# Eight layers over 625 nodes in one kernel: waits of the TensorE queue are rearranged, and three rows of the soft mixture go by DMA

## The chip, the cores and the metric

The kernel runs on one core of a Trainium2 chip, as one launch. The time is device time in microseconds (us) from the start to the end of an execution; of several runs the median counts. A core has five engines with an instruction queue each: TensorE (PE, matrix products and transposes), VectorE (DVE), ScalarE (ACT), GpSimd (POOL) and SyncE (SP), which here only issues DMAs. An engine works through its own queue in order and waits on semaphores for the others.

## The reference, cut to what matters

Eight residual layers act on x, 625 nodes by 768 features in float32, over one graph of 5000 drawn edges, their reverses and self-loops. Each layer reads a LayerNorm of x and adds its result to x:

- L0_gnn: graph attention, 12 heads of 64
- L0_ffn: mixture of 8 experts with hidden size 192, each node takes two
- L1_gnn: one graph convolution
- L1_ffn: self-attention with 12 heads and a mixture of 8 experts with biases (top 2)
- L2_gnn: two graph convolutions
- L2_ffn: soft mixture, 4 experts of 1024 slots each
- L3_gnn: two graph attention layers, 4 heads of 512, then one of 768
- L3_ffn: mixture of 8 experts (top 2)

Two pieces are needed below. Graph attention takes, for each target node, the softmax over its edges of a leaky ReLU:

```python
e = jax.nn.leaky_relu(a1[src] + a2[dst], negative_slope=NEG_SLOPE)
m = jax.ops.segment_max(e, dst, num_segments=n)
w = jnp.exp(e - m[dst])
```

The soft mixture takes two softmaxes of the same logits, one over the nodes for each slot (dispatch), one over all slots for each node (combine):

```python
dispatch = jax.nn.softmax(logits, axis=1)
combine = jax.nn.softmax(logits.reshape(B, N, E * S), axis=-1).reshape(B, N, E, S)
slots = jnp.einsum('bnd,bnes->besd', x, dispatch)
```

## The kernel before, in words

The 625 nodes are five tiles of 125 (TILES[t], P = 125, NT = 5); 768 features are six chunks of 128 (KD). x stays in SBUF for the whole kernel. PSUM is one pool of four buffers of two banks each (self.ps()); whoever asks for a fifth waits until the oldest has been read. Weights go through a pool `w` of four buffers; SP loads them in order, each as soon as PE has finished with the buffer. The instructions of each engine are put in order by a scheduler that goes by its own estimates; the order of the calls in the code is its start, and it may move an instruction ahead of others that it doesn't depend on.

**Products.** Nearly every large product is done with seven products of half size in place of eight. `half_products` and `half_nodes`, `right_sums` and `left_sums` make the sums that go in; L401 and L385 (in `half_mm` and `half_rest`) and the `add` of `tile_pair` and `down` take the products out of PSUM, on DVE, with one copy U on ACT (L384, L1178) at the start. So after PE's first product, the next ones need a PSUM buffer that DVE or ACT has read.

**Entering a layer.** `final(t)` adds a bias where there is one and normalises tile t: `ln_tile` takes bn_stats on DVE (L167), bn_aggr (L170), a square root on ACT (L171), a reciprocal (L172), a scale (L174, L180), all into xn. `turned` then transposes xn on PE (L187), and `turn_tile` copies it to xT (L191, or with a scale and a shift per feature L194, six copies on ACT). `late` and `turn_due` hold a tile's transposes back until a later point.

**L0_gnn.** The edge counts are in AT (625 x 625). `log_counts` takes their logarithm, `mask_tile` transposes a tile of AT (five transposes, L531), and ACT makes a mask mb (L534) and the degree (L535) from it. A loop over i (12 heads and 4 more) then runs five steps on different heads: `gat_largest(i)` spreads a row of a1 over all partitions (`spread`: five transposes of a broadcast column, L132), takes on DVE the largest a1 among each target's neighbours (L560, five times) into gat_m, and makes of it on POOL the largest logit gat_u (L565 to L569); `gat_exp(i - 2)` spreads gat_u, subtracts it on DVE (L582) and exponentiates on ACT (L584); `back(i - 4)` and `gather(i - 3)` are PE's products (L118, copied by ACT at L826) and their way out; `score(i)` makes the scores of a head on ACT (L547) and POOL (L551). A small copy on ACT (L813) makes head i's scores wait for gat_m of head i - 1; after the loop L906 makes the copy of the identity wait for the last gat_u.

**The mixtures.** `experts` runs up the hidden chunks c = 0, 2, ... 10 (hg), takes the gates from the router's logits, writes them as 8 rows to DRAM (gD, L1072) and reads each back spread over 128 partitions (L1031, L1034), and multiplies them in (L1041). `gate_parts` (L958 to L965) splits the gates into three bfloat16 parts for the expert biases, only in L1_ffn. `down` multiplies by the second weights: tile 0 alone, then the pairs t = 1 and t = 3 with seven products each, in the order 1, 6, 7, 4, 2, 5, 3. Where another layer follows, `final(0)` stands behind product 6 of t = 1. `beside` runs small steps beside a mixture (in L0_ffn and L1_ffn the attention vectors of L3_gnn: a load av_w on SP and two dot products on DVE, L1354 and L1355): one per c in the loop upwards and seven behind the products of t = 1.

**L2_ffn.** A loop over i (16 pairs of 128 slots; e = i // 4 - 1 is the expert before, q = i % 4) makes the logits of a pair (`front`, seven products, L347), their largest per slot, the exponentials (L1722, on ACT), turns these (L1735) and multiplies (`hidden`). When an expert's four pairs are there, `largest(e)` transposes the running maximum M and reduces it to rm (125 nodes on partitions by 5 tiles by 4 experts, L1765). In the next step, between the products of `front`, `spread(e)` makes a row of it on 128 partitions (five transposes L132, a copy on ACT L1770), `weights(e, q)` subtracts that row from a pair on DVE (L1774) and exponentiates it on ACT, four times, and `combine(e)` multiplies the result by hE (the products of hE and lt, L125).

**L3_gnn.** `narrow` (L268 to L277) makes the attention ends of all heads: products with a narrow matrix, a copy on ACT (L273), five transposes (L276), a reduction on DVE. `project(h)` makes a head's features with `tile_pair`, which takes `between`, a function that runs between its products 1, 2 and 6, 7. `right_sums` here is POOL's for heads 2 and 3.

## Time and profile before

| | us |
|---|---|
| median of 3 runs (lowest to highest) | 1891.52 (1891.14 to 1892.33) |
| the profiled execution | 1890.76 |
| its span, from the first instruction to the last | 1889.0 |
| mean granted TensorE clock in it | 0.985 |

Where the layers lie in the span, and how long PE was busy in each (read from the busy times by stretch; the ends are chosen by hand at the first instructions of the next layer):

| stretch | us | PE busy | PE clock |
|---|---|---|---|
| L0_gnn | 0 to 229 | 191.02 | 0.89 |
| L0_ffn | 229 to 380 | 146.12 | 0.99 |
| L1_gnn | 380 to 450 | 70.00 | 1.00 |
| L1_ffn, attention | 450 to 703 | 248.22 | 1.00 |
| L1_ffn, mixture | 703 to 862 | 151.56 | 1.00 |
| L2_gnn | 862 to 1040 | 178.00 | 1.00 |
| L2_ffn | 1040 to 1400 | 356.47 | 1.00 |
| L3_gnn | 1400 to 1700 | 296.96 | 1.00 |
| L3_ffn | 1700 to 1889 | 183.47 | 1.00 |

How to read the profile lines: a line of the timeline or of a group names the engine, the line of the kernel, the operation, the tile written and the tiles read, the shape and the count. Behind it stands in brackets how long the engine had been idle, and which instruction released it. The list of waits sums the idle time by the pair of waiting line and releaser. "SPq" is SyncE's queue, where a DMA is issued. Matmul ends are modelled, so PE's busy time includes some pipelining. The clock is the share of full TensorE speed that the throttle granted.

### The profile page before, as it was taken

How to read it: one execution, taken by the hardware profiler on the slowest of the kernel's cores; microseconds unless marked ns; L12 is line 12 of the kernel's file. 1: busy time of each engine (PE TensorE's matmuls, PEld its weight loads, DVE VectorE, ACT ScalarE, POOL GpSimd, SP SyncE). 2: the span in 40 equal slices, each digit the busy share in tenths (PEclk: the TensorE clock that was granted, in tenths of full speed). 3: DMA queues.
4: the chain of work that ended last, by engine and by line, in shares of the span. 5: the costliest groups of instructions: out<-in, count | busy, mean ns of one | idle time of the engine just before them, and what ended most of it. 6: DMA issues, size and time to landing. Idle time of an engine off the chain costs nothing.

```text
span 1889.0 us, 21692 instructions
## 1 busy us (share of the span) xinstructions
PE 1821.8 (96%) x8224; PEld 1270.4 (67%) x8224; DVE 1112.4 (59%) x2211; ACT 528.2 (28%) x963; POOL 658.4 (35%) x556
## 2 busy tenths in 40 slices
PE   8969899999999999999999999999999999999998
PEld 7844565555677766655555778878767888556765
DVE  8789856547566765674936464555756555144452
ACT  2479721002254533100110131322314233111200
POOL 0079665234410044743106322231235321401551
PEclk9968999999999999999999999999999999999999
DMA  2040142210200024414420211001011122021321
GB/s 70 22 145 34 40 116 70 78 58 27 92 25 26 1 70 153 127 53 140 138 67 34 76 43 59 26 26 34 6 39 35 40 72 67 1 73 52 94 72 33
DMA packets 69637, 115.03 MB, mean 61 GB/s; under 512 B 8189, under 2 KB 38111, under 8 KB 69534
## 3 DMA queue, kind: packets, MB, share of 16 engines
q1 hardware_dynamic: 69274, 113.57, 18.9%
q8 instruction: 65, 1.06, 0.2%
q14 instruction: 38, 0.31, 0.1%
q10 hardware_dynamic: 260, 0.09, 0.0%
HBM read 111.63 MB, written 2.01 MB: 60 GB/s over the span
## 4 chain that ended last, share of the span: by engine, by line
PE 84%; DVE 8%; ACT 2%; DMA 2%; issue 2%; POOL 1%; SPq 0%; ACTq 0%; DVEq 0%; POOLq 0%
PE ps L125 65%; PE ps L118 4%; PE ps L768 2%; PE ps L1889 2%; PE ps L1518 2%; PE ps L1550 2%; PE ps L1537 1%; PE ps L187 1%; POOL gat_w L551 1%; PE ps L132 1%; DVE gat_w L582 1%; PE ps L1735 1%; DMA x<-in_x 1%; PE ps L706 1%; DVE av_junk L1355 1%
## 5 line engine op out<-in xcount | busy, mean ns | idle before, releaser
L327 POOL TENSOR_TENSOR S<-w 128x384 f32<-128x384 f32 x40 | 41.4, 1040 | 401.9 <-PE ps L125 298.9
L125 PE MATMUL ps<-xT,w 128*128 128x313 f32 x480 | 137.6, 427 | 0.7 <-ACT pr L1526 0.7
L125 PE MATMUL ps<-w,xT 128*125 128x384 f32 (+2 forms) x392 | 125.2, 473 | 0.0
L125 PE MATMUL ps<-T,w 128*128 128x313 f32 x408 | 122.0, 430 | 0.9 <-DVE U L401 0.9
L551 POOL TENSOR_TENSOR gat_w<-gat_w,xT 125x625 f32<-125x625 f32 x60 | 86.2, 1469 | 102.8 <-DVE xT L523 96.5
L125 PEld LDWEIGHTS ps<-xT,w 128*128 128x128 f32 x480 | 89.3, 189 | 33.6 <-ACT pr L1526 0.9
L125 PE MATMUL ps<-T,S 128*128 128x313 f32 x348 | 103.8, 432 | 1.7 <-DVE T L307 1.4
L125 PEld LDWEIGHTS ps<-w,xT 128*125 128x125 f32 x392 | 72.8, 188 | 46.2 <-issue 11.1
L125 PE MATMUL ps<-xT,S 128*128 128x313 f32 x336 | 100.9, 429 | 2.1 <-DVE hg L401 2.1
L125 PE MATMUL ps<-w,S 128*125 128x384 f32 x292 | 99.8, 487 | 2.6 <-DVE x L1170 2.6
L125 PEld LDWEIGHTS ps<-T,w 128*128 128x128 f32 x408 | 75.6, 189 | 32.2 <-issue 1.8
L125 PE MATMUL ps<-w,hg 128*125 128x384 f32 x288 | 96.3, 486 | 0.0
L125 PE MATMUL ps<-hh,gat_w 125*125 125x257 f32 (+1 forms) x400 | 89.8, 379 | 0.0
L125 PE MATMUL ps<-w,x2T 128*125 128x384 f32 (+1 forms) x280 | 84.2, 449 | 0.0
L125 PEld LDWEIGHTS ps<-T,S 128*128 128x128 f32 x348 | 64.0, 189 | 28.7 <-ACT lt L355 4.4
L125 PEld LDWEIGHTS ps<-w,S 128*125 128x125 f32 x292 | 54.5, 188 | 42.4 <-DVE x L1170 3.9
L125 PEld LDWEIGHTS ps<-hh,gat_w 125*125 125x125 f32 x400 | 73.4, 187 | 11.3 <-issue 0.4
L125 PEld LDWEIGHTS ps<-xT,S 128*128 128x128 f32 x336 | 62.1, 189 | 26.6 <-POOL hg L1041 2.5
L118 PE MATMUL ps<-gat_w,ft 125*65 125x500 f32 (+1 forms) x240 | 74.9, 471 | 4.4 <-DVE gat_w L582 3.1
L125 PEld LDWEIGHTS ps<-w,hg 128*125 128x125 f32 x288 | 53.6, 188 | 36.6 <-issue 0.6
L1355 DVE CUSTOM_DVE_ANT_0 av_junk<-av_w,av_a 128x512 f32<-128x512 f32 (+1 forms) x80 | 74.1, 926 | 6.4 <-DMA av_w<-in_L_gnn_W 4.1
L560 DVE CUSTOM_DVE_ANT_0 junk<-ps,mb 125x625 f32<-125x625 f32 x85 | 68.5, 806 | 13.9 <-PE ps L132 9.9
(459 smaller groups left out, 3794.7 us busy)
## 6 DMA issues: line engine op xcount, KB each, us to landing
w<-in_L_ffn_phiT SPq DMA_DIRECT2D x8, 1536.0 KB
w<-in_L_gnn_W SPq DMA_DIRECT2D x8, 1536.0 KB
gate<-gD SPq DMA_DIRECT2D x24, 312.5 KB
w<-in_L_ffn_w SPq DMA_DIRECT2D x6, 1152.0 KB
w<-in_L_gnn_W SPq DMA_DIRECT2D x6, 1152.0 KB
av_w<-in_L_gnn_W SPq DMA_DIRECT2D x24, 256.0 KB
av_w<-in_L_gnn_W SPq DMA_DIRECT2D x16, 384.0 KB
w<-in_L_ffn_w SPq DMA_DIRECT2D x3, 1536.0 KB
```

Source lines behind the costliest of these rows:

```text
L118: self.nc.tensor.matmul(pv[:, s, :], lhs[i], rhs[i][:, s, :], start=i == 0, stop=i == n - 1)
L125: self.nc.tensor.matmul(out, lhs[i], rhs[i], start=i == 0, stop=i == n - 1)
L132: self.nc.tensor.transpose(pv[:, t, :], col(t).to_broadcast([P, rows]), self.ident[:P, :P])
L187: nc.tensor.transpose(pv[:, k, :P], src[:, k * 128 : (k + 1) * 128], self.ident[:P, :P])
L327: nc.gpsimd.tensor_tensor(S1, A21, A22, ALU.add)
L551: nc.gpsimd.tensor_tensor(w[:, s, :], w[:, s, :], lc[:, s, :], ALU.add)
L560: nc.vector.tensor_tensor_reduce(self.n3(junk), row, self.n3(mb[:, t, :]), 1.0, -3e38, ALU.subtract, ALU.max, m[:, t : t + 1],)
L768: nc.tensor.matmul(acc[j // 2][:, j % 2, :], ohs[:, TILES[j]], ohd[:, 0:HN], start=c == cs[0], stop=c == cs[-1],)
L1355: nc.vector.tensor_tensor_reduce(junk, wt, row, 1.0, 0.0, ALU.mult, ALU.add, dst)
L1518: nc.tensor.matmul(sv[r][:, s, :], qk[half[r], 0, TILES[t]], self.n3(qk[half[r], 1, :])[:, s, :], start=True, stop=True,)
L1550: nc.tensor.matmul(ov[half[r]], v[:, s, h * DH : (h + 1) * DH], pT[r][:, s, :], start=s == 0, stop=s == NT - 1,)
L1889: nc.tensor.matmul(pv[:, j, :], zTs[t][:, k, :], w2[k // 3][:, k % 3, js], start=k == 0, stop=False,)
```

## The change

The change has these parts:

- `gat_largest`: the four operations on POOL become two on DVE, and a row that was made before can be handed in. L0_gnn spreads head 0's row between the log counts and the mask tiles.
- `ln_tile` gets `behind`: a one-column copy on ACT ahead of the square root, which has to wait for what it reads. `down` hands in a column that is written after U2 (one more small copy on ACT), for t = 1.
- `down` calls `beside` behind its adds, once each (`dots`), once in t = 1 and four times in t = 3, in place of seven times behind t = 1; the loop upwards calls two steps at c = 4 and c = 8.
- `turn_tile` with a scale (only L1_ffn's norms) gives three of the last tile's six copies to DVE.
- `gate_parts` goes from DVE to POOL.
- `right_sums` gets `last`: in L1_ffn's v, the last of the four sums goes to POOL.
- In L2_ffn, `spread` of experts 0 to 2 writes a column set of rm to DRAM and reads it back as a row on 128 partitions, both issued on SP, directly behind `largest`. Expert 3 keeps the transposes.
- `narrow` returns its second half as a function, which runs further back: in L3_gnn's first layer between products 1, 2 and 6, 7 of the second pair, with two mask tiles behind it, in the second layer behind another product.

The diff, cut to its core:

```diff
-    def ln_tile(self, src, dst, scale=None, st=None, act=False):
+    def ln_tile(self, src, dst, scale=None, st=None, act=False, behind=None):
...
         nc.vector.bn_aggr(mv, st)
+        if behind is not None:
+            nc.scalar.copy(rs, behind)
         nc.scalar.activation(rs, mv[:, 1:2], AF.Sqrt, bias=self.eps[:P])
         nc.vector.reciprocal(rs, rs)
         if scale is not None:
...
             nc.scalar.copy(dst[:, :, TILES[t]], pv[:, :, :P])
             return
         for k in range(KD):
+            if t == NT - 1 and k % 2:
+                nc.vector.tensor_scalar(
+                    dst[:, k, TILES[t]], pv[:, k, :P], scale[:, k : k + 1], bias[:, k : k + 1],
+                    ALU.mult, ALU.add,
+                )
+                continue
...
     def narrow(self, pool, chunks, w, cols, dst):
         nc, n, few = self.nc, len(chunks), w
...
         hT = pool.tile([128, N], F32, tag="narrow", name="narrow", bufs=1)
         nc.scalar.copy(self.n3(hT), pv)
-        pv = self.nv(self.ps(), P, 128)
-        for t in range(NT):
-            nc.tensor.transpose(pv[:, t, :], hT[:, TILES[t]], self.ident)
-        nc.vector.tensor_reduce(
-            dst, pv.rearrange("p t (q e) -> p t e q", q=4)[:, :, 0:cols, :], AX.X, ALU.add
-        )
+        def turned():
+            pv = self.nv(self.ps(), P, 128)
+            for t in range(NT):
+                nc.tensor.transpose(pv[:, t, :], hT[:, TILES[t]], self.ident)
+            nc.vector.tensor_reduce(
+                dst, pv.rearrange("p t (q e) -> p t e q", q=4)[:, :, 0:cols, :], AX.X, ALU.add
+            )
+        return turned
...
-    def right_sums(self, T, q, eng=None):
+    def right_sums(self, T, q, eng=None, last=None):
         eng = eng or self.nc.vector
...
         eng.tensor_tensor(T3, B22, B12, ALU.subtract)
         eng.tensor_tensor(T2, T3, B11, ALU.add)
         eng.tensor_tensor(T4, B21, T2, ALU.subtract)
-        eng.tensor_tensor(T1, B12, B11, ALU.subtract)
+        (last or eng).tensor_tensor(T1, B12, B11, ALU.subtract)
         return B11, B21, B22, T4, T1, T2, T3
...
-    def gat_largest(self, pool, mb, a1, a2):
+    def gat_largest(self, pool, mb, a1, a2, row=None):
         nc = self.nc
-        row = self.spread(lambda t: a1[:, t : t + 1], P)
+        if row is None:
+            row = self.spread(lambda t: a1[:, t : t + 1], P)
         m = self.small.tile([P, NT], F32, tag="gat_m", name="gat_m")
         for t in range(NT):
             junk = pool.tile([P, N], F32, tag="junk", name="junk", bufs=1)
...
                 m[:, t : t + 1],
             )
         u = self.small.tile([P, NT], F32, tag="gat_u", name="gat_u")
-        nc.gpsimd.tensor_tensor(u, m, a2, ALU.add)
-        v = self.small.tile([P, NT], F32, tag="gat_v", name="gat_v")
-        nc.gpsimd.tensor_scalar(v, u, 0.8, 0.0, ALU.mult, ALU.max)
-        nc.gpsimd.tensor_scalar(u, m, 0.2, None, ALU.mult)
-        nc.gpsimd.tensor_tensor(u, u, v, ALU.add)
+        nc.vector.scalar_tensor_tensor(u, a2, 0.8, m, ALU.mult, ALU.add)
+        nc.vector.scalar_tensor_tensor(u, m, 0.2, u, ALU.mult, ALU.max)
         return m, u
...
             tmpp = ctx.enter_context(tc.tile_pool(name="g0tmp", bufs=1))
             for s in range(NT):
                 self.log_counts(lc, s)
+            row = self.spread(lambda t: al[:, t, 0, 0:1], P)
             for t in range(NT):
                 self.mask_tile(mb, t, act=True)
             self.prepare(router="L0_ffn_router")
...
             for i in range(H + 4):
                 if i < H:
-                    ms[i], us[i] = self.gat_largest(tmpp, mb, a1[i], a2[i])
+                    ms[i], us[i] = self.gat_largest(
+                        tmpp, mb, a1[i], a2[i], None if i else row
+                    )
                 if 0 <= i - 2 < H:
                     h = i - 2
                     self.gat_exp(
...
         nc, lg = self.nc, self.lg
         r = self.small.tile([P, NT, NEXP], F32, tag="gr", name="gr", bufs=1)
-        nc.vector.tensor_copy(r[:, 0, 0:1], after)
+        nc.gpsimd.tensor_copy(r[:, 0, 0:1], after)
         parts = gb[:, :, 0, 0 : 3 * NEXP].rearrange("p t (e i) -> p t e i", i=3)
...
         for j in range(1, gb.shape[2]):
-            nc.vector.tensor_copy(gb[:, :, j, 0 : 3 * NEXP], gb[:, :, 0, 0 : 3 * NEXP])
+            nc.gpsimd.tensor_copy(gb[:, :, j, 0 : 3 * NEXP], gb[:, :, 0, 0 : 3 * NEXP])
...
                 )):
                     gate(o)
                 if beside and c < NF:
-                    beside(1, hg[:P, c + 1, 0:1])
+                    beside(2 if c in (4, 8) else 1, hg[:P, c + 1, 0:1])
             up_pool.close()
             with tc.tile_pool(name="moedown", bufs=1) as dp:
                 self.down(dp, a[w2], hg, gT3, (b2p, b2n) if b2 else None, after, beside)
...
             x11, x12, x21, x22 = (
                 x[:, o, j * HD : (j + 1) * HD] for o in (t, t + 1) for j in range(2)
             )
+            def dots(n, after):
+                if beside and n in ((5,) if t == 1 else (1, 2, 3, 4)):
+                    beside(1, after[:, 0:1])
             U = pool.tile([P, 2, HD], F32, tag="U", name="U")
             U2, U3 = U[:, 0], U[:, 1]
             prod(1, a1)
             nc.scalar.copy(U2, a1)
+            if after and t == 1:
+                nc.scalar.copy(U3[:, 0:1], U2[:, 0:1])
             add(x11, U2)
+            dots(1, x11)
             prod(6, a2)
             add(U2, U2, a2)
+            dots(2, U2)
             if after and t == 1:
-                self.final(0)
+                self.final(0, behind=U3[:, 0:1])
             prod(7, b1)
             add(U3, U2, b1)
             add(x12, U2)
+            dots(3, x12)
             prod(4, b2, (t + 1, bl))
             if t == 1:
                 sums(3)
...
             if not after:
                 store(t, 0)
             add(x22, U3)
+            dots(4, x22)
             prod(5, a2, (t + 1, br))
             add(x22, a2)
             if not after:
                 store(t + 1, 1)
             add(x12, a2)
+            dots(5, x12)
             prod(3, b1, (t, br), (t + 1, bn))
             add(x12, b1)
...
                 continue
             for o in (t, t + 1):
                 self.final(o, hold=True)
-            if beside and t == 1:
-                beside(7, U3[:, 0:1])
...
                     [wv[j][:, k, :] for k in range(KD)],
                 )
             nc.vector.tensor_tensor(halves(v[:, 0, :]), pv, halves(vb), ALU.add)
-            rights = self.right_sums(vp, columns(wv))
+            rights = self.right_sums(vp, columns(wv), last=nc.gpsimd)
             lefts = {1: self.left_sums(vp, yT, 1, inplace=False)}
...
                     nc.vector.tensor_reduce(rm[:, :, e], tv, AX.X, ALU.max)
                 def spread(e):
-                    bv = self.spread(lambda t: rm[:, t, e : e + 1], 128)
                     rows[e] = mp.tile([128, N], F32, tag="mrow", name="mrow")
-                    nc.scalar.copy(self.n3(rows[e]), bv)
+                    if e == E:
+                        bv = self.spread(lambda t: rm[:, t, e : e + 1], 128)
+                        nc.scalar.copy(self.n3(rows[e]), bv)
+                        return
+                    r = rD[e : e + 1, :]
+                    nc.sync.dma_start(r.rearrange("o (t p) -> p (o t)", p=P), rm[:, :, e])
+                    nc.sync.dma_start(rows[e], r.to_broadcast([128, N]))
+                E = NE - 1
+                dram = c1.enter_context(
+                    tc.tile_pool(name="f2d", bufs=1, space=bass.MemoryType.DRAM)
+                )
+                rD = dram.tile([E, N], F32, name="rD")
                 def weights(e, q):
                     pr = pairs[4 * e + q]
...
                     )
-                E = NE - 1
...
                     o = 2 * i - 2
                     c = [[], [], []]
                     if e >= 0 and q == 1:
-                        c[0] += [(spread, e), (weights, e, 0), (weights, e, 1)]
+                        c[0] += [(weights, e, 0), (weights, e, 1)]
                         c[1] += [(weights, e, 2)]
                         c[2] += [(weights, e, 3)]
                     if 0 < i < LAST - 1:
...
                     largest_slots(i)
                     if e >= 0 and q == 0:
                         largest(e)
+                        spread(e)
                     if e >= 0 and q == 1:
                         combine(e)
                 load()
...
                     nc.vector if h < 2 else nc.gpsimd,
                 )
                 for i, t in enumerate((1, 3)):
+                    behind = None
                     if i < len(between):
-                        between[i](T)
+                        behind = between[i](T)
                     self.tile_pair(
                         T[:P, 3 * HK], lefts[t], rights,
-                        [hh[h][:, o, c, 0:HH] for o in (t, t + 1) for c in range(2)],
+                        [hh[h][:, o, c, 0:HH] for o in (t, t + 1) for c in range(2)], behind,
                     )
             def scores(h):
...
             def second(T):
                 self.turn_due(NT - 1)
-                self.narrow(tp, [xT[:, k, :] for k in range(KD)], self.v1, 2 * H, ends)
+                turned = self.narrow(tp, [xT[:, k, :] for k in range(KD)], self.v1, 2 * H, ends)
                 sums_of(3, None)
-                for t in range(3, NT):
-                    self.mask_tile(mb, t)
+                def behind():
+                    turned()
+                    for t in range(3, NT):
+                        self.mask_tile(mb, t)
+                return behind
             project(0, first, second)
...
                 )
             nc.scalar.copy(h2[:, 0, :, 0:384], self.hv(p, P))
             turn(*todo.pop(0))
-            self.narrow(tp, chs, self.v2, 2, c)
+            turned = self.narrow(tp, chs, self.v2, 2, c)
             w = gw.tile([P, NT, N], F32, tag="gat_w", name="gat_w")
             spare = gw.tile([128, NT * N], F32, tag="gat_w", name="spare")
...
                 add(C[t][2], C[t][2], p)
             prod(lambda t: A[t][0], B11, one, (1,))
+            turned()
             self.gat_scores(w, c1, self.spread(lambda t: c2[:, t : t + 1], P), lc)
             _, u = self.gat_largest(tp, mb, c1, c2)
             prod(lambda t: A[t][0], B11, one, (3,))
```

More of the change, by code (lines that the diff above doesn't have):

```diff
@@ L957, in gate_parts @@
         r = self.small.tile([P, NT, NEXP], F32, tag="gr", name="gr", bufs=1)
-        nc.vector.tensor_copy(r[:, 0, 0:1], after)
+        nc.gpsimd.tensor_copy(r[:, 0, 0:1], after)
         parts = gb[:, :, 0, 0 : 3 * NEXP].rearrange("p t (e i) -> p t e i", i=3)
-        nc.vector.tensor_copy(parts[:, :, :, 0], lg)
-        nc.vector.tensor_tensor(r, lg, parts[:, :, :, 0], ALU.subtract)
-        nc.vector.tensor_copy(parts[:, :, :, 1], r)
-        nc.vector.tensor_tensor(parts[:, :, :, 2], r, parts[:, :, :, 1], ALU.subtract)
+        nc.gpsimd.tensor_copy(parts[:, :, :, 0], lg)
+        nc.gpsimd.tensor_tensor(r, lg, parts[:, :, :, 0], ALU.subtract)
+        nc.gpsimd.tensor_copy(parts[:, :, :, 1], r)
+        nc.gpsimd.tensor_tensor(parts[:, :, :, 2], r, parts[:, :, :, 1], ALU.subtract)
         for j in range(1, gb.shape[2]):
-            nc.vector.tensor_copy(gb[:, :, j, 0 : 3 * NEXP], gb[:, :, 0, 0 : 3 * NEXP])
+            nc.gpsimd.tensor_copy(gb[:, :, j, 0 : 3 * NEXP], gb[:, :, 0, 0 : 3 * NEXP])
     def experts(self, over_all, w1, w2, gelu, b1=None, b2=None, after=None, beside=None):
```

## The prediction

> **What bounds the kernel now.** I read the page first: the busy times, and the shares of the chain that ended last.
>
> ```profile
> PE 1821.8 (96%) x8224; PEld 1270.4 (67%) x8224; DVE 1112.4 (59%) x2211; ACT 528.2 (28%) x963; POOL 658.4 (35%) x556
> ...
> PE 84%; DVE 8%; ACT 2%; DMA 2%; issue 2%; POOL 1%; SPq 0%; ACTq 0%; DVEq 0%; POOLq 0%
> ```
>
> TensorE (PE) is busy for 1821.8 of 1889.0 us and carries 84% of the chain. An edit can therefore earn two things: PE work removed, or part of the 67.2 us in which PE stands. So the second view was the list of PE's waits (who released it, us in total, times, longest):
>
> ```profile
> PE ps L132 <- POOL gat_u L569: 10.1, 3, 6.2
> PE ps L125 <- ACT U L1178: 5.0, 2, 2.6
> ...
> PE ps L125 <- DVE x L1170: 2.6, 2, 1.5
> ...
> PE ps L125 <- DVE hg L401: 2.1, 1, 2.1
> ...
> PE ps L276 <- ACT narrow L273: 1.6, 2, 0.8
> PE ps L125 <- DVE T L307: 1.4, 3, 0.9
> ...
> PE ps L187 <- DVE xn L180: 1.3, 1, 1.3
> ```
>
> These seven rows are 24.1 us, and each ends at an instruction that the change moves, shortens or gives to another engine. A third view, busy time by stretch, shows where PE isn't the limit: from 140 to 175 us PE is busy 31.98 of 35, DVE 32.33, ACT 33.80, POOL 32.16. Layer 0's head loop is a ring of four engines; everywhere else PE's queue sets the pace.
>
> Times below are those of the profiled execution, 1890.76 us (span 1889.0); the median, 1891.52, is 0.76 higher, and I carry differences over unchanged.
>
> **Layer 0's attention: gat_largest and the first row.** Four POOL operations (L565 198 ns, L567 247, L568 233, L569 197; 1.1 to 1.2 us as a chain) become two on DVE, 17 times. A comparable 125x5 row on DVE (L844) takes 0.19, with a pitch of some 0.12. The 10.1 us of gat_u waits are not all won, as what is late next is DVE:
>
> ```profile
> 103.84 0.81 DVE L560 CUSTOM_DVE_ANT_0 junk<-ps,mb 125x625 f32<-125x625 f32 x1 [2.01 <-PE ps L132]
> ...
> 111.26 3.41 DVE L582 TENSOR_TENSOR gat_w<-gat_w,ps 125x3125 f32<-125x3125 f32 x1 [0.95 <-POOL gat_w L551]
> ```
>
> Head 0's maxima (L560) begin at 103.84 because their row's five transposes stand behind all mask transposes. Moved ahead, they can begin with the first mask tile at 100.15; ACT makes one each 1.36 us (L534 and L535), the fifth at 105.6, so the maxima end near 106.5, not 108.42: -1.9. The first L582 then waits for POOL's L551s, which lose four small operations in between (1.1). I take -2.5 at the loop's start. In the steady loop one head takes 8.70 us: five exponentials on ACT (3.55), L826 0.66, L813 0.19, then DVE's last L560 0.74 and L582 3.44, and 0.13 of hand-over. DVE idles 0.56 per head just ahead of the first L560, which takes two steps of 0.12: nothing lost, and if that slack weren't there, 12 x 0.24 = 2.9 would be. At the loop's end ACT waits 1.20 at 202.88 for POOL's gat_u; half of it goes: -0.6. Sum **-3.1**. Bounds: -1 if only the hand-over goes, -6 if the DVE gaps of 3.09 at 141.15 and 0.84 at 128.40 shrink too. Both end at transposes queued behind a gather, in a stretch of PE clock 0.66. In layer 3 the same edit ends a PE gap of 0.56 at 1450.42: **-0.5**.
>
> **The two down projections, L0_ffn and L1_ffn.** The copy U2 is queued on ACT behind final(0)'s Sqrt, which waits for DVE's statistics:
>
> ```profile
> 323.00 0.21 DVE L170 BATCH_NORM_AGGREGATE lt_mv<-lt_st 125x2 f32<-125x12 f32 x1
> 323.24 0.29 ACT L171 ACTIVATE lt_r<-lt_mv,eps 125x1 f32<-125x1 f32 x1 [18.50 <-DVE lt_mv L170]
> ...
> 323.63 0.48 ACT L1178 COPY U<-ps 125x384 f32<-125x384 f32 x1
> ...
> 324.17 2.25 PE L125 MATMUL ps<-Td,S 128*125 128x384 f32 x4 [2.64 <-ACT U L1178]
> ```
>
> With the Sqrt held behind U2, PE waits for the copy alone: 0.48 and 0.1 of hand-over in place of 2.64, so -2.0; and for the second MoE 2.31 becomes 0.6, -1.7. The Sqrt, with two tiny copies before it, runs some 0.5 later; its tile is transposed at 333.05, 9 us on: hidden. After the first gap PE runs 3.4 us at a granted 0.5 (matmul pitch 0.64 against 0.32), some five matmuls, 1.6 us; I count -1.3, since a gap of 0.6 may still bring it. The seven attention-vector steps (L1355, 0.69 each and two DMA waits, 1.18 and 0.32) that held up L1170 are spread over calls before: the gaps of 1.53 (344.42) and 1.12 (829.3) go, -2.5. DVE has room at the new places (it idles 4.92 at 325 to 330). Their loads now stand ahead of L1_gnn's second weight load on SP; that one is issued at 372.2, when PE frees its buffer, some 11 us after the last such load could wait, so nothing; were it later than that, PE would stand us for us. Sum **-7.0** for a full effect (2.0 + 1.3 + 1.7 + 2.5 = 7.5, less 0.5 for the tiny copies and new DVE steps); at least -4, if the burst only moves.
>
> **L1_ffn's small edits.** Between 744.9 and 751.4 DVE runs the gate's parts while PE waits for L401:
>
> ```profile
> 748.29 1.49 DVE L961 TENSOR_TENSOR gr<-lg,gb 125x40 f32<-125x40 f32 x1
> ...
> 750.07 0.98 DVE L963 TENSOR_TENSOR gb<-gr,gb 125x40 bf16<-125x40 f32 x1
> ...
> 751.30 0.47 DVE L401 TENSOR_TENSOR hg<-U,ps 128x313 f32<-128x313 f32 x1
> ```
>
> On POOL they cost some 2 us (the 125x5 rows there take 0.2, these are 8 times wider) and are read by PE near 765: PE's 2.05 at 751.91 goes, **-1.8** (0 if POOL is late). The last tile's six copies (0.34 each on ACT) go half to DVE, which idles there: PE's 0.87 at 726.25 becomes 0.2, **-0.6**. The last right sum of v (1.34 on DVE, L438) to POOL, some 3 us there and needed near 468: the LayerNorm behind it is 1.3 earlier, PE's 1.28 at 463.77 goes, **-1.1** (0 if POOL's is needed before).
>
> **L2_ffn: rows by DMA.** Per expert 0 to 2 it takes five transposes from PE (pitch 0.109, so 0.55; 1.64 in all) and a copy from ACT (0.68), and adds a write of 625 maxima and a broadcast read of 312.5 KB, both on SP. No row shows a write of single elements. The nearest is the gate's round trip, write then dependent read:
>
> ```profile
> 253.76 0.30 SPq L1072 DMA_DIRECT2D gD<-gT  x1
> 255.35 0.33 SPq L1031 DMA_DIRECT2D gate<-gD  x1
> ```
>
> 1.6 us between the issues, and 2.3 to 3.9 more until a gate lands: the row is there 4 to 6 us after rm. Nothing else is issued on SP within 10 us of it. DVE's order is what waits:
>
> ```profile
> 1117.67 0.81 DVE L1765 TENSOR_REDUCE rm<-ps 125x5 f32<-125x640 f32 x1
> ...
> 1120.68 1.45 DVE L1774 TENSOR_TENSOR lt<-lt,mrow 128x1250 f32<-128x1250 f32 x1
> ```
>
> rm ends at 1118.48; L1774 starts 2.2 later now, and 4 to 6 later then. From landing, four L1774 and three L347 between them take 7.2, the last exponential 1.35. PE wants that pair some 13.8 after rm (the products of hE and lt begin at 1131.79, this pair comes seventh). So it holds to a landing of 5.3; beyond that each us costs one, per expert. At 5, PE gains 0.55 less 0.2 behind the second Exp: -0.35 each, **-1.0** in all. Bounds: -1.6, and +14 if all 625 elements went through one DMA engine at the 9 ns that this trace's 4-byte packets take (5.6 us more: landing near 10.5, +5.2 less 0.55, three times). I take the value of the gate's row. The Trainium skill speaks against this part: "DMA: Bandwidth & Descriptors", section "Rules for kernel authors", says that a strided last dimension becomes one descriptor per element, as rm[:, :, e] is. Its section on the anatomy of one DMA gives about 2.0 us of fixed cost for each, most of it the write's receipt; by that figure alone an estimate of the row is 4 us and the sum stays -1.6 to -1.0. The row's 1.6 is a little under the figure, and no run here shows the elements.
>
> **narrow() in L3.** PE no longer waits for the copy L273 (0.68): six products stand between. 0.83 + 0.80 go; the head scores behind it come 1.6 later, while PE still has projections to do: **-1.4**.
>
> **Sum.** -3.1 - 0.5 - 7.0 - 1.8 - 0.6 - 1.1 - 1.0 - 1.4 = -16.5, so 1891.5 - 16.5 = **1875.0**.
>
> **Rivals.** (1) The stalls move. When the wait on U2 is gone, the next product may meet the next late sum, as every product there needs a buffer that an L1170 on DVE must have read first; a new wait then takes the old one's place. For it: DVE is busy 25.59 of 30 us (110 to 140) and 32.33 of 35 (140 to 175) in layer 0's loop. Against it: beside the MoEs it is busy 16.59 of 25 (320 to 345) and 13.54 of 20 (810 to 830). With half of each term: 1883. (2) Layer 0 gives more: its granted clock is 0.66 from 110 to 140, and PE gaps of 3.36 and 6.16 come before; without them the first two gathers (7.38 and 8.08) could take the 5.43 of the one at 158.75, -4.6, and the spreads between them some -1.4: 1869. Against it: the ring, not PE, sets the period. (3) The slow side: the row's write is element by element and lands late. Each us beyond 5.3 stalls L1774, so the PSUM buffers behind it, so PE, three times. All else is -15.5; to end over 0.2% slower it needs 7 us of stall per expert, a landing 12.3 after rm or later (12 ns per element on one engine). At 14: +8.2 x 3 - 15.5, 1900. Against it: 125 rows need not share one engine. (4) The scheduler undoes the order, or a tiny copy doesn't hold the Sqrt: only L0_gnn, the gate's parts and L3 remain, 1883 as well.
>
> **Chances.** Forecast (1870 to 1881) 0.60; (1) and (4) together 0.20, of which 0.05 within 0.2% (3.8 us, about what a measurement of this kernel tells from no change); (2) 0.11; (3) 0.09: 0.02 faster, 0.02 within, 0.05 slower. So faster 0.88, within 0.07, slower 0.05. The range leaves out half of (2) and all of (3) that isn't faster: 1866 to 1885.
>
> **What would show it.** In the profile after: no L132 wait on gat_u, the first L582 near 109; U L1178 ending PE's wait under 0.7; no wait on x L1170, hg L401 or narrow; PE's busy time lower by some 3 (transposes and clock); the first L1774 some 5 after rm without a PE wait behind it. Wrong would be: PE waits on lt L1774 or pairs' Exp, POOL ending PE's waits at 465 or 765, or L0_gnn ending where it does now.

## The result and the profile after

The changed kernel takes 1922.9 us (median of 4 runs, 1920.79 to 1923.39), beside 1891.33 before: a ratio of 1.0163, with a 95% interval of 1.0147 to 1.0179. It is 31.6 us slower, where 16.5 us less were forecast. The profiled execution took 1923.39 us with a span of 1921.7; the stretches below are from it and from the profiled execution before (1889.0), so their sum is 32.7.

To place the loss, take a milestone that both kernels have, the start of the LayerNorm aggregates (L170 in both), and note how much later each comes than before. Differences between milestones, us (e5 and e11 are two of the experiments below):

| stretch | changed | both costly parts undone (e5) | rows by five runs (e11) |
|---|---|---|---|
| L0_gnn | -0.2 | -0.3 | -0.6 |
| L0_ffn, upwards | +10.7 | -0.3 | -0.6 |
| L0_ffn, down, to L1_gnn | -5.0 | -5.2 | -5.2 |
| L1_gnn and attention | -1.4 | -1.3 | -1.5 |
| L1_ffn's mixture, upwards | +11.0 | -1.4 | -1.4 |
| its down part, to L2_gnn | -3.2 | -3.3 | -3.3 |
| L2_gnn and L2_ffn | +22.6 | +0.1 | -0.4 |
| L3_gnn and L3_ffn | -1.7 | -1.4 | -1.6 |

So most of what was forecast came, and three stretches lost 44 us beside it. The row of L0_gnn is of single executions: in the eleven profiled kernels that have this code there, its end came between 2.9 us earlier and 0.2 later than in the profile before. The page after, busy times and chain (shares of the span by engine, then by line):

```profile
PE 1830.1 (95%) x8209; PEld 1273.8 (66%) x8209; DVE 1145.5 (60%) x2251; ACT 526.0 (27%) x958; POOL 649.8 (34%) x496
...
PE 82%; DVE 8%; DMA 4%; ACT 3%; issue 2%; POOL 1%; SPq 0%; ACTq 0%; DVEq 0%; POOLq 0%
```

The chain has 4% of DMA in place of 2%: transfers now end waits that no transfer ended before. PE has 15 instructions fewer and is busy 8.3 us longer: behind seven of its nine new waits matmuls ran at half the granted clock for a while (the last section has the numbers). The list of PE's waits:

```profile
PE ps L125 <- DVE lt L360: 17.7, 3, 6.5
PE ps L125 <- DVE U L414: 16.9, 6, 6.4
...
PE ps L132 <- DVE gat_u L582: 9.0, 2, 6.0
...
PE ps L125 <- DVE U L1187: 1.5, 2, 1.1
```

The rows for ACT's U copy (5.0), x (2.6), hg (2.1), narrow (1.6) and xn (1.3) are gone, as forecast; T (1.4) stayed, and behind the same adds as x PE now waits 1.5 for U (L1187). Two new rows stand at the top, 34.6 us in nine waits. Both name DVE, and in both DVE was itself held up. The timeline of L2_ffn behind the first row maxima shows the first (DVE, SP and PE, from separate views):

```profile
1129.45 0.81 DVE L1793 TENSOR_REDUCE rm<-ps 125x5 f32<-125x640 f32 x1
...
1140.74 1.46 DVE L1814 TENSOR_TENSOR lt<-lt,mrow 128x1250 f32<-128x1250 f32 x1 [6.27 <-DMA mrow<-rD]
1142.12 0.47 DVE L360 TENSOR_TENSOR lt<-lt,ps 128x312 f32<-128x312 f32 x1
```

```profile
1130.33 0.29 SPq L1802 DMA_DIRECT2D rD<-rm  x1
1136.59 0.34 SPq L1803 DMA_DIRECT2D mrow<-rD  x1
```

```profile
1137.28 2.12 PE L125 MATMUL ps<-xw,Dn 125*128 125x192 f32 x12
1144.80 2.45 PE L125 MATMUL ps<-xT,w 128*128 128x313 f32 x4 [5.40 <-DVE lt L360]
```

The dependent read is issued 6.26 us after the write, and DVE has the row 10.5 us after rm is done (1130.25); for the next two experts it is 7.02 and 6.72, and 11.6 and 10.9. DVE's queue has the subtraction L1814 ahead of the sums L360 that read PSUM. While L1814 waits for the row, PE runs out of PSUM buffers at 1139.40, and stands 5.40 us. The next four matmuls take 2.45 us; six of this size took 1.74 ahead of the wait.

The second is in the mixtures' upward loop, at c = 4. Here is DVE around the two vector steps, with PE's next product (timeline, all engines):

```profile
272.37 0.08 DVE L1383 DVE_READ_ACCUMULATOR2_ANT v<- 128x1 f32 x1
...
274.77 1.48 DVE L1383 CUSTOM_DVE_ANT_0 av_junk<-av_w,av_a 128x512 f32<-128x512 f32 x1 [2.32 <-DMA av_w<-in_L_gnn_W]
...
276.18 0.47 DVE L398 TENSOR_TENSOR hg<-U,ps 128x313 f32<-128x313 f32 x1
...
276.58 1.59 DVE L1383 CUSTOM_DVE_ANT_0 av_junk<-av_w,av_a 128x512 f32<-128x512 f32 x1
...
278.10 0.47 DVE L414 TENSOR_TENSOR U<-U,ps 128x313 f32<-128x313 f32 x1
...
278.71 1.91 PE L125 MATMUL ps<-T,w 128*128 128x313 f32 x3 [5.36 <-DVE U L414]
```

The second step waits 2.32 us for its weight row and then runs two dot products, and L398 and L414, for which PE waits, are queued among them. At c = 4 of L1_ffn PE's wait is longer (6.43) and the load's part smaller (1.40). There one dot product lasts 4.22 us, while POOL runs one operation after the other; where POOL is idle, all 20 of this size in the changed kernel take 0.68 or 0.69:

```profile
762.75 0.95 DVE L1383 CUSTOM_DVE_ANT_0 av_junk<-av_w,av_a 128x512 f32<-128x512 f32 x1 [1.40 <-DMA av_w<-in_L_gnn_W]
...
764.02 4.22 DVE L1383 CUSTOM_DVE_ANT_0 av_junk<-av_w,av_a 128x512 f32<-128x512 f32 x1
764.59 1.50 POOL L1058 TENSOR_TENSOR hg<-hg,gate 128x625 f32<-128x625 f32 x1
766.05 1.64 POOL L1073 TENSOR_TENSOR b2t<-b2t,b2p 96x768 f32<-96x768 f32 x1
```

### The profile page after: what moved, and what is told of

Same layout as the page of the kernel before. It is cut to its first block, busy times and chain, and to the rows that moved or that the text cites. A ratio compares the mean times of both kernels' runs of the same rounds, so it can differ in the third digit from the quotient of the medians.

```text
span 1921.7 us, 21632 instructions
## 1 busy us (share of the span) xinstructions
PE 1830.1 (95%) x8209; PEld 1273.8 (66%) x8209; DVE 1145.5 (60%) x2251; ACT 526.0 (27%) x958; POOL 649.8 (34%) x496
## 4 chain that ended last, share of the span: by engine, by line
PE 82%; DVE 8%; DMA 4%; ACT 3%; issue 2%; POOL 1%; SPq 0%; ACTq 0%; DVEq 0%; POOLq 0%
PE ps L125 64%; PE ps L118 4%; PE ps L781 2%; PE ps L1928 2%; PE ps L1546 2%; PE ps L1578 2%; PE ps L1565 1%; PE ps L189 1%; DVE gat_w L595 1%; DMA av_w<-in_L_gnn_W 1%; DMA rD<-rm 1%; DVE av_junk L1383 1%; DMA x<-in_x 1%; DVE junk L575 1%; PE ps L132 1%
## 5 line engine op out<-in xcount | busy, mean ns | idle before, releaser
L125 PE MATMUL ps<-xT,w 128*128 128x313 f32 x480 | 142.8, 440 | 18.5 <-DVE lt L360 17.7
L125 PE MATMUL ps<-T,w 128*128 128x313 f32 x408 | 126.8, 442 | 16.9 <-DVE U L414 16.9
L1383 DVE CUSTOM_DVE_ANT_0 av_junk<-av_w,av_a 128x512 f32<-128x512 f32 (+1 forms) x80 | 85.4, 1067 | 6.8 <-DMA av_w<-in_L_gnn_W 4.8
L781 PE MATMUL ps<-ohd,ohs 125*125 125x313 bf16 x425 | 65.1, 308 | 9.5 <-DVE ohs L774 9.5
```

The source lines that it names most:

```text
L125: self.nc.tensor.matmul(out, lhs[i], rhs[i], start=i == 0, stop=i == n - 1)
L781: nc.tensor.matmul(acc[j // 2][:, j % 2, :], ohs[:, TILES[j]], ohd[:, 0:HN], start=c == cs[0], stop=c == cs[-1],)
L1383: nc.vector.tensor_tensor_reduce(junk, wt, row, 1.0, 0.0, ALU.mult, ALU.add, dst)
```

## The experiments

All are variants of the changed kernel, each timed beside the kernel before (its median was 1890.2 to 1890.5 in these).

**e1: the rows on PE again.** The diff against the changed kernel:

```diff
+                    bv = self.spread(lambda t: rm[:, t, e : e + 1], 128)
                     rows[e] = mp.tile([128, N], F32, tag="mrow", name="mrow")
+                    nc.scalar.copy(self.n3(rows[e]), bv)
-                    nc.sync.dma_start(r.rearrange("o (t p) -> p (o t)", p=P), rm[:, :, e])
-                    nc.sync.dma_start(rows[e], r.to_broadcast([128, N]))
...
-                        c[0] += [(weights, e, 0), (weights, e, 1)]
+                        c[0] += [(spread, e), (weights, e, 0), (weights, e, 1)]
```

> The changed kernel with the rows of experts 0 to 2 made by five transposes and a copy again, at their old place. Theory (the write of 625 single elements makes the row land some 10.5 us after rm, and DVE's subtraction holds the sums behind it): L2_ffn, which is 22.6 us longer than before the change, is as before, so 1922.9 - 22.6 = 1900.3, and the PE waits on lt L360 (17.7 us in three) are gone. Rival (the new order of the products around the spread costs, not the row): the stretch stays over 10 us longer than before, 1910 or more.

Measured: 1899.48, 23.4 less than the changed kernel, and L2_ffn as before to 0.1 us. The waits on L360 are gone. The rows by DMA cost 23 us; the rest of the loss lies elsewhere.

**e2: the write in runs of 20 bytes.**

```diff
-            rm = big.tile([P, NT, NE], F32, name="rm")
+            rm = big.tile([P, NE, NT], F32, name="rm").rearrange("p e t -> p t e")
...
-                    nc.sync.dma_start(r.rearrange("o (t p) -> p (o t)", p=P), rm[:, :, e])
+                    nc.sync.dma_start(r.rearrange("o (p t) -> p (o t)", p=P), rm[:, :, e])
...
+                    rv = rows[e].rearrange("q (p t) -> q t p", t=NT)
+                        p4, p4, rv.unsqueeze(1).to_broadcast([128, 2, NT, P]), ALU.subtract
```

> The changed kernel with rm laid out so that the write has 125 runs of 20 bytes in place of 625 single elements; the row then has another order of nodes, and DVE reads it with a stride. Theory (the elements make the write long): the dependent read is issued 1.6 to 2.2 us after the write in place of 6.26, the first L1814 starts some 6 after rm in place of 10.5, the stalls shrink from 6 to about 1 each: L2_ffn 4 to 7 us longer than before the change in place of 22.6, so 1904 to 1908. Rival 1 (what a write to DRAM and its receipt cost, whatever the pieces): read issued 6 us after as now, 1922 to 1924. Rival 2 (the strided read on DVE costs): L1814 longer than 1.45.

Measured: 1913.11. SP's and DVE's timelines in this kernel:

```profile
1128.76 0.28 SPq L1802 DMA_DIRECT2D rD<-rm  x1
1130.32 0.34 SPq L1803 DMA_DIRECT2D mrow<-rD  x1
```

```profile
1134.07 2.44 DVE L1816 TENSOR_TENSOR lt<-lt,mrow 128x1250 f32<-128x1250 f32 x1 [1.18 <-DMA mrow<-rD]
```

The dependent read is issued 1.56 us after the write in place of 6.26, with the same bytes, the same queue and the same DRAM. So the single elements made the write long, by 4.7 us, or 7.5 ns for each of the 625 (twelve such writes in four kernels took 5.8 to 7.0 us, the three here 1.5 to 1.6). The second rival holds as well: with a stride of 20 bytes the subtraction takes 2.44 in place of 1.45, four times per expert. L2_ffn is still 16.8 us longer than before, and the time missed the expected one. The stride fits as the reason: the L360 that ends PE's wait is done 5.9 us after the first subtraction starts, in place of 4.0, and PE stands 2.25 to 2.31 us per expert, each time with slow matmuls behind. No run changes the stride alone.

**e3: one vector step per c upwards.** The two steps taken out go behind adds of the down part:

```diff
-                    beside(2 if c in (4, 8) else 1, hg[:P, c + 1, 0:1])
+                    beside(1, hg[:P, c + 1, 0:1])
...
-                if beside and n in ((5,) if t == 1 else (1, 2, 3, 4)):
+                if beside and n in ((4, 5) if t == 1 else (1, 2, 3, 4, 5)):
```

> The changed kernel with one vector step per c in the loop upwards again; the two steps taken out go into the down part, one more behind an add of t = 1 and of t = 3. Theory (the second step at c = 4 and 8 waits on its load, which lands behind a weight load, and its dot products run 1.4 to 1.6 us each beside POOL, while PE waits for the sums queued behind it on DVE): PE's waits on U L414 (16.9 us in six) fall under 2, and with the clock dips behind them 16 to 19 us go; the two added steps in down cost 0 to 2: 1904 to 1908. Rival (the gate loads, moved on SP among the others, are what is late): the waits stay, 1918 or more.

Measured: 1898.4, 24.5 less than the changed kernel, more than expected. The waits on U L414 fell from 16.9 to 1.4 us, the upward stretches to +0.1 and -1.2, and down lost nothing by its two further steps. L0_gnn ended 1.5 us earlier in this execution than in the changed kernel's; the next but one experiment says why that is no effect of the edit.

**e6: a third buffer for the vectors' weight rows**, with both steps at c = 4 and c = 8 kept. This asks whether the load or DVE's queue made the wait:

```diff
-                    wt = pool.tile([128, cols], F32, tag="av_w", name="av_w", bufs=1 + which)
+                    wt = pool.tile([128, cols], F32, tag="av_w", name="av_w", bufs=3)
```

> The changed kernel with three buffers for the vectors' weight rows in place of two, so that the second step's load is issued before the mixture's weight load. Theory (of the 5.4 us wait at c = 4 only 2.3 is the load, the rest is two more dot products of 1.4 to 1.6 us in DVE's queue): two waits at c = 4 shrink from 5.4 and 6.4 to 3 to 4, those at c = 8 (2.1) stay: 5 to 7 us less than the changed kernel, 1916 to 1918. Rival (the load is the whole cause): 14 or more go, 1908 or less.

Measured: 1907.64, 15.3 less. My theory failed and the rival held in size, though not wholly: the wait at c = 4 fell from 5.4 to 1.9 and from 6.4 to 1.8, those at c = 8 stayed.

```profile
PE ps L125 <- DVE U L414: 8.8, 6, 2.2
```

With two buffers the second row's load is issued at 266.75, 2.9 us behind a weight load of 1152 KB on SP (263.86) and with two gate loads between, and DVE has it at 274.8, 8 us later. The third buffer lets it go before them. In L1_ffn the dot products then run earlier too, beside other operations of POOL, and the longest takes 1.36 us in place of 4.22. The waits make 8.1 of the 15.3 (16.9 less 8.8). The rest is about what the clock had cost: matmuls behind all four waits over 2 us in the changed kernel ran at half pitch for a while, which cost some 7.2 us (half of the time PE ran at that clock), and in this kernel none did:

```profile
304.71 2.51 PE L125 MATMUL ps<-T,w 128*128 128x313 f32 x6 [2.09 <-DVE U L414]
```

```profile
298.56 1.82 PE L125 MATMUL ps<-T,w 128*128 128x313 f32 x6 [2.08 <-DVE U L414]
```

The first line is from the changed kernel, the second from this one, both behind the same wait at c = 8. What remains against one step per c (e3: 1898.4) is 9 us, most of it these waits (8.8 against 1.4): the second step's dot products in DVE's queue.

**e4: gat_u on POOL again**, head 0's row left early.

```diff
-        nc.vector.scalar_tensor_tensor(u, a2, 0.8, m, ALU.mult, ALU.add)
-        nc.vector.scalar_tensor_tensor(u, m, 0.2, u, ALU.mult, ALU.max)
+        nc.gpsimd.tensor_tensor(u, m, a2, ALU.add)
...
+        nc.gpsimd.tensor_tensor(u, u, v, ALU.add)
```

> The changed kernel with gat_u made by four operations on POOL again; head 0's row stays early. Theory (a DVE step of this kind waits for POOL's running operation, 1.35 us at every second head of the loop, and so takes back what the start gained): the loop's period is 8.70 again, L0_gnn ends some 1.5 us earlier than in the changed kernel, L3_gnn 0.5 later: 1922, within 1 us. Rival (the steps are free and POOL's chain is what costs): L0_gnn ends 1 to 2 us later, 1924.5.

Measured: 1920.93. From one subtraction of gat_u to the next (L582 before, L595 in the changed kernel, L598 here) the loop took 8.70 to 8.81 in its steady part, where the changed kernel took 8.60 and 9.49 in turn; before it was 8.70. So the theory on the loop holds. From its first subtraction to its last the loop took 99.6 to 99.9 us in the three profiled kernels with gat_u on POOL (before, e4, e7), and 101.0 to 102.4 in the eleven with it on DVE. The time doesn't settle it alone: the first of these operations starts between 108.3 and 109.7 us in the changed kernel and e1 to e4, a scatter as large as the effect.

**e5: both costly parts undone** (e1 and e3 together).

> The changed kernel with both costly parts undone: rows by transposes, and one vector step per c upwards (the two others in down). Theory (the two causes are apart in time and add): 1922.9 - 23.4 - 24.5 = 1875.0, 16 us faster than before, with no PE wait over 3 us after 230 us in the span. Rival (the parts share a loss, for example the clock): 1880 or more.

Measured: 1876.44, a ratio of 0.9922 (0.9905 to 0.9939) to the kernel before, within 1.4 of the sum. The two causes are apart in time and add.

**e7: e5 with gat_u on POOL.**

> As the kernel with both parts undone, and gat_u on POOL again, head 0's row early. Theory (DVE's short steps wait for POOL's running operation): the loop of 12 heads keeps 8.7 to 8.8 per head in place of 8.6 and 9.5 in turn, L0_gnn 1 to 2 us shorter, L3_gnn 0.5 longer: 1873 to 1874.5. Rival (steps on DVE are worth their place): 1876.

Measured: 1876.32, the same as e5. The shorter loop and L3_gnn's 0.8 us (1.1 gained in e5, 0.3 here) weigh each other out: where gat_u is made earns nothing that the time shows.

**e8: rows by DMA from five runs of 500 bytes**, with one vector step per c. PE transposes rm's 125 x 5 once, and ACT copies 5 x 125:

```diff
-                    nc.sync.dma_start(r.rearrange("o (t p) -> p (o t)", p=P), rm[:, :, e])
+                    tv = self.ps()[0:NT, 0:P]
+                    nc.tensor.transpose(tv, rm[:, :, e], self.ident[:P, :P])
+                    r5 = mp.tile([NT, P], F32, tag="r5", name="r5", bufs=1)
+                    nc.scalar.copy(r5, tv)
+                    nc.sync.dma_start(r.rearrange("o (t p) -> (o t) p", p=P), r5)
```

> One vector step per c upwards, and the rows of experts 0 to 2 by DMA, but from a transposed 5 x 125 copy: five runs of 500 bytes, one small transpose and copy more, DVE's subtraction of the row as in the changed kernel. Theory (what hurts is the write by elements; the landing may be 5.3 us after rm before it costs): landing near 6.3 after rm, 1 us of stall per expert less 0.44 of transposes: 1875 + 2 = 1877, within 2. Rival (DVE's order around the row costs by itself): 1882 or more.

Measured: 1887.6, on the rival's side. The trace shows a third cause, though: no wait on L360 is left, and a new one stands at the head of PE's list.

```profile
PE ps L1803 <- DVE rm L1793: 9.2, 3, 3.1
```

I had put the small transpose directly behind `largest`, where PE had nothing queued while rm was reduced.

**e11: e8 with the transpose at the old place**, behind other products (`(spread, e)` in c[0], as in e1).

> As the rows by five runs of 500 bytes (1887.6), with the small transpose at the place of the old five, behind other products on PE. In the run before PE stood 3.07 us ahead of each small transpose, as its rm was not reduced yet, and no longer waited for DVE's sums, with the row 6.6 us after rm. Theory (a row some 6.6 after rm costs nothing, only the write by elements and that wait did): PE's three waits go, 1875 to 1877. Rival (DVE's order around a row that comes by DMA costs): 1880 or more.

Measured: 1874.68, a ratio of 0.9917 (0.9902 to 0.9932), 1.8 below e5, with the intervals overlapping. DVE's timeline in it:

```profile
1105.20 0.81 DVE L1793 TENSOR_REDUCE rm<-ps 125x5 f32<-125x640 f32 x1
...
1112.13 0.48 DVE L360 TENSOR_TENSOR lt<-lt,ps 128x312 f32<-128x312 f32 x1 [1.95 <-PE ps L125]
1112.53 0.47 DVE L360 TENSOR_TENSOR lt<-U,ps 128x312 f32<-128x312 f32 x1
1112.92 2.82 DVE L1818 TENSOR_TENSOR lt<-lt,mrow 128x1250 f32<-128x1250 f32 x2
```

The subtraction starts 6.9 us after rm and waits for no DMA. Two more L360 now stand ahead of it, in the scheduler's order. So a row by DMA that is there 6.9 us after rm costs nothing, and what it earns beside the transposes is not clear of the noise. Whether a row from single elements, there 10 us after rm, would cost less in this order was not run.

**e9 and e10: what the down part gained.** e5 without `behind`, and e5 with the seven steps in one burst:

```diff
-                self.final(0, behind=U3[:, 0:1])
+                self.final(0)
```

> The kernel with both costly parts undone (1876.4), and final(0)'s square root free to run ahead of the copy U2 again. Theory (the copy behind the square root cost PE 2.64 and 2.31 us and one clock dip): PE's two waits on ACT's copy come back, 4 to 5.5 us more: 1880.5 to 1882. Rival (the gain in down came from the spread vector steps alone): 1877 or less.

Measured: 1882.93, 6.5 above e5, more than expected. The wait is back in full, in its old size:

```profile
PE ps L125 <- ACT U L1200: 5.0, 2, 2.6
```

The two stretches lost 4.2 and 2.3 us against e5. The first lost more than its wait of 2.65, as matmuls at half pitch followed that wait, as they did before the change.

```diff
-                if beside and n in ((4, 5) if t == 1 else (1, 2, 3, 4, 5)):
+                if False:
...
+            if beside and t == 1:
+                beside(7, U3[:, 0:1])
```

> The kernel with both costly parts undone, and the seven vector steps of each down part in one burst behind t = 1 as before the change. Theory (the burst held up the adds of t = 1: gaps of 1.53 and 1.12): 2 to 4 us more, 1878.5 to 1880.5. Rival (spread steps cost as much as the burst): 1876.5 within 1.

Measured: 1879.99, 3.6 above e5. The wait on x is back, and longer than its 2.6 before:

```profile
PE ps L125 <- DVE x L1187: 5.9, 2, 3.0
```

**e12: e5 with three buffers** for the vectors' rows.

> The kernel with both costly parts undone, and three buffers for the vectors' weight rows. The third buffer took 15.3 us from the changed kernel, so the load was the larger part of the wait at the second steps, against what I expected. Theory (with one step per c nothing waits for a load but 1.1 us in down): 1875 to 1876.5. Rival (loads issued earlier collide with the weight and gate loads): 1878 or more.

Measured: 1875.36. With one step per c the third buffer earns 1.1 us, and the intervals overlap.

## Why the prediction was wrong

**The rows by DMA: the wrong end of a range.** The prediction bounded this by -1.6 and +14 and took the row of the gate's round trip, 1.6 us from write to dependent read. The write took 6.26. The step that failed is "I take the value of the gate's row": that write has eight runs of 2500 bytes, this one 625 of 4. The other end of the range had the size: a landing near 10.5 us after rm and 5.2 us of stall per expert; measured were 10.5 to 11.6, and 5.4, 6.5 and 5.8. Its reason was another, though, and that it came so near is luck. It let all elements pass one DMA engine, 9 ns each. Here is the DMA of the first write, its busy share in tenths in 40 equal slices from 1130.3 to the read at 1136.59:

```profile
DMA  0000004444200000000000000000000000000000
...
DMA packets 630, 0.00 MB, mean 0 GB/s; under 512 B 630, under 2 KB 630, under 8 KB 630
```

All 630 packets lie between 1131.2 and 1132.0, far closer than one engine at 9 ns each could bring them (5.7 us). Then no packet moves until the read goes out 4.6 us later. What the write does in that time the trace doesn't show; e2's 125 runs do without it.

Of the 8.6 us by which the 22.6 exceed the 14, the longer stalls are 2.1 (17.7 in place of 15.6) and the clock some 5.4, as each stall was followed by about six matmuls at half pitch; about 1 us is left without a cause. The bound of 5.3 us for the landing was right in size for this order of DVE's queue, by another mechanism. PE ran out of PSUM buffers 9.15 us after rm (1139.40), and the L360 that frees the next one ends 4.0 after the first L1814 starts, so a row 5.1 after rm would have been in time; it was not the exponentiated pair that PE missed. With another order (e11) 6.9 costs nothing.

The prediction cited a warning and put it aside. The Trainium skill's page "DMA: Bandwidth & Descriptors", section "Rules for kernel authors", says that a strided last dimension is lowered to one descriptor per element and advises a contiguous one. The traces agree: 630 packets for 625 elements, and in e2 the same 2500 bytes in runs of 20 bytes were through 4.7 us earlier. The figure of about 2.0 us per DMA, which the prediction took from that page's section "Anatomy of one DMA — SWDGE (gpsimd) path", stands there for DMAs that GpSimd issues. These are issued on SP, and the writes in runs took 1.2 to 1.6 us to the dependent read.

**The vector steps upwards: a term that was left out.** The prediction looked for cover in down ("DVE has room at the new places") and asked on SP's queue only about the load for L1_gnn. The two places at c = 4 and c = 8 had no price. They cost 10.7 and 11.0 us. Two things in the profile before could have told: the dot products there took up to 1.6 beside POOL where 0.69 was counted, and a load is issued only when its buffer falls free, there behind a weight load of 1152 KB and gate loads. e6 puts the larger part on the late load, about half of that through the clock, and e3 takes all of it away. How much of the rest is the POOL operation beside a dot product and how much DVE's queue was not separated.

**Layer 0's attention: the steps were mis-sized.** Forecast -3.1 with two steps of 0.12. The loop did start 1.7 earlier, and PE's wait on gat_u moved to DVE rather than going (9.0 in place of 10.1). But L582 took 1.35 at every second head:

```profile
155.59 3.17 POOL L565 TENSOR_TENSOR gat_w<-gat_w,xT 125x625 f32<-125x625 f32 x2
155.76 1.35 DVE L582 SCALAR_TENSOR_TENSOR gat_u<-gat_m,gat_u 125x5 f32<-125x5 f32 x1
```

It starts 0.17 us after one POOL operation and ends at 157.11, 0.02 after that one ends (157.09, the first of the two). The slack of 0.56 was gone, the heads took 9.05 on average in the steady part, and from the first subtraction to the last the loop took 101.6 in place of 99.6, so the 1.7 was given back. The second end of the prediction's own price, 2.9 if the slack weren't there, was the nearer one. The row that says so was in the prediction: L961, a 125x40 operation of 1.49 us on DVE, was read as a cost of its place, not as a cost of POOL.

**What was right.** Down: forecast -7.0, measured -8.2 (-5.0 and -3.2); e9 and e10, each taking one part out of e5, put 6.5 on `behind` and 3.6 on the spread steps. v's last sum on POOL: the first milestone behind it moved by -1.9, of which 0.5 came back, for -1.1. The gate's parts on POOL: the wait on hg is gone and the stretch 1.4 shorter in e5, for -1.8. narrow and gat_u in L3: -1.7 for -1.9. turn_tile's half on DVE earned nothing: PE's wait on T at the second norm is 0.87 as before. Without the three costly stretches the forecast sum would have been near: e5 took 1876.4, e11 1874.7, where 1875.0 was forecast. Part of that is luck: layer 0 and turn_tile gave less than their terms, down more (8.5 in e5).

**The chances** gave the slow side 0.05, and its rival named one of the two causes with the right price. It said that a landing 12.3 us after rm was needed to end over 0.2% slower, as all other gains stood against it. A landing of 9.9 to 10.8 was enough: with the vector steps undone and the rows still slow the kernel takes 1898.4 (e3), 0.4% more than before, since the stalls and the clock behind them cost more than was counted. That a second loss of the same size would come beside it was not thought of. In rival (4) the terms that are named add up to 6.8, so to 1884.7 rather than 1883; nothing rests on it.

## What to carry to other kernels

Price a DMA by the number of its runs: a column out of a wider tile is one run per element, and a small transpose or another layout of the tile makes five or 125 of them. Before a small step goes into an in-order queue, list what it waits for (its load, and what that load is queued behind) and which instruction behind it another engine needs; a second buffer more may be cheaper than another place. When two rows of the profile price a term an order apart, ask which of them has the shape of the new operation, and not which has its name.

## What the runs showed of the hardware

In this kernel a short DVE operation with two inputs in SBUF that begins while POOL runs a tensor_tensor ends only when that one does. The two new steps on 125x5 (L581, L582) took 0.15 to 0.17 us in the 12 cases of the changed kernel in which POOL ran nothing. The 22 that began beside a POOL operation took 0.17 to 1.44, and 21 of them ended 0.02 to 0.03 us after it; the last had 0.1 to wait and ended 0.07 after it. L575 in the same stretch, which takes its row from PSUM, kept its 0.80. Here is one of the cases, in L3_gnn:

```profile
1474.88 1.25 DVE L581 SCALAR_TENSOR_TENSOR gat_u<-ends,gat_m 125x5 f32<-125x5 f32 x1
1476.16 1.43 DVE L582 SCALAR_TENSOR_TENSOR gat_u<-gat_m,gat_u 125x5 f32<-125x5 f32 x1
...
1477.53 1.81 POOL L449 TENSOR_TENSOR Tw<-w 128x768 f32<-128x768 f32 x1
```

L582 ends at 1477.59, as POOL passes from one operation to the next (1477.53 to 1477.57). That DVE and POOL share something which one holds for a whole operation fits these; the traces don't show what it is. The Trainium skill's page "SBUF — State Buffer", section "SBUF: two separate sides", says that GpSimd's port pair is shared with VectorE and is an exclusive lock for a whole instruction; a DVE operation with two SBUF inputs takes it against a GpSimd operation that reads SBUF. Both new steps read two tiles from SBUF, POOL's operations beside them read SBUF as well, and the traces agree.

The length of a PE wait alone did not tell whether the clock fell. Behind L0_gnn every wait over 4.5 us, in all these kernels, was followed by matmuls at half pitch (0.52 for 0.26 us), in a stretch of 3.4 or 6.8 us with a granted clock of 0.50. Shorter waits went both ways: 2.09 and 2.19 in the changed kernel were followed by one, 2.08 and 2.18 at the same places of e6 were not; 2.64 before the change and 2.65 in e9 were, while 2.31 before the change and 3.02 in e10 were not. At half the clock a matmul takes twice its time, so half of the time for which PE ran in such a stretch is lost: 1.5 to 2.3 us behind each of the seven waits in the changed kernel. A wait of 5.4 us cost about 7 there.
